# A three-layer hybrid on one core: the residual kept in the output and added to by the last stores, with the filter loop's buffers, filter banks and frequency chunks laid out anew

## Chip, cores and metric

The kernel runs on one core of one Trainium2 chip. The metric is device time of one execution in microseconds (us), the median over several runs. All numbers are float32.

## The reference, cut to what matters

The input is x of 8 × 32 × 32 × 128, which is 8 sequences of 1024 tokens with 128 channels. Three layers run over it, each adding to its input: an attention layer (4 heads of 32), a state-space layer that runs forwards and backwards, and a spectral filter layer (STU). The change touches the end of the second layer and the third. The third layer takes the normalised tokens u and computes, beside three taps of regression on u, a causal convolution of u with 16 spectral filters, each followed by a 128 × 128 matrix, once with u and once with u of alternating sign:

```python
U_plus, U_minus = _stu_conv(phi, u, PADDED_SL)          # FFT convolution, K = 16 filters
s = sigma ** SIGMA_POW
out = jnp.einsum('btkd,k,kde->bte', U_plus, s, Mpp)
out = out + jnp.einsum('btkd,k,kde->bte', U_minus, s, Mpm)
...
out = out + jnp.einsum('btd,de->bte', ui, Mu[i])        # three taps, i = 0..2
```

Which of four banks of matrices is used follows from a gate, and so does a mask `keep` over the positions.

## The kernel before, in words

Everything that counts stands in `fast_kernel` (`general_kernel` runs only if a check on the attention's denominators fails). X[b], the tokens of sequence b with all that has been added to them so far, lives in SBUF, 4 KB per partition, for all 8 sequences.

**Order of the work.** A tile framework places buffers in pools and inserts waits. A buffer that is laid on the bytes of an earlier one waits for the earlier one's last reader, and that may be a store. Within a `manual_schedule` the engines named in it run in program order: in the state-space part all five engines (`ALL_IN_ORDER`), in the two filter stages TensorE, VectorE, ScalarE (ACT) and GpSimd (POOL) (`IN_ORDER`), while SP, which issues nearly all DMAs, is ordered by the framework.

**First filter stage** (L1558 to L1627), a loop over b from 2 to 8. For each sequence `transform(b)` turns the normalised tokens by TensorE (`cpt`, L561), computes their spectra at 128 frequencies as matrix products (`pf`, L571; copied by ACT, L579; summed by VectorE and POOL, L582 to L589) and stores them to `ud` in DRAM (L592). `taps_of(b - 1, k)` computes the regression for each half k (`pu`, L601), and VectorE adds it into X (L611). `store_residual` (L614) then stores X[b] to the DRAM tensor `xa`. In between, `turned(n)` for n = 0 to 3 brings one quarter of the filter matrices (8 of 32, `md`) into SBUF (L1568), turns it on TensorE (`mdt`, L1573), copies it (L1574), and stores it to `me` in DRAM (L1577). After the fourth, four DMAs (L1580) load `me` with the filter index on partitions, as `mst`. Sequences 0 and 1 have had the same done to them earlier, within the state-space part, and X[7] is re-loaded in another layout by `reload(u)` at L1542.

**Second filter stage** (L1629 to L1744), a loop over c, 16 chunks of 8 frequencies. `matrices(c + 1, n, ...)`, for n = 0 to 7, makes the chunk's 128 × 128 matrices from `taps` and `mst`: 16 products into four PSUM banks (`pg`, L1644), which VectorE (L1655) and ACT (L1657) copy by turns into `gs`. `loaded_spectra` (L1664) loads the chunk's spectra `u`, and POOL makes a second form of them (L1667, L1668). `apply` multiplies spectra and matrices (`py`, L1678), `gather` forms sums on ACT and VectorE (L1693 to L1699) and stores them to `yd` (L1701), 4 frequencies per store, so that partition p of the sums is one (frequency, block, sequence, part). `fetch(c)` (L1709) brings the first part of what the tail reads back into `early_yt`, with the frequency on partitions. TensorE's order within an iteration is: two groups of the next chunk's `matrices`, one `apply`, four times. Both `gs` and `u` come from a pool of two buffers that is opened after the first stage's pools and X are released, so that gs0 lies on bytes of X.

**Tail** (L1747 to L1784). When the last chunk begins, `load_residuals` (L1712) brings part of the residuals `xa` back to SBUF; the rest follows in the tail. Six loads of 1 MB (L1753, `room<-yd`) bring the frequencies' sums, partition = frequency. For each of four pieces (block, half of the sequences) VectorE forms z (L1759), TensorE applies the inverse transform (`pz`, L1769), VectorE multiplies by `keep` and adds the residual (L1776), and ACT's queue issues the store to `out` (L1779); the last piece is stored in two parts.

The frequencies have the order 1, 3, 5, ...: `odd` (L326) counts them on one row, and `alt` (L393) holds a sign that alternates from one to the next.

Of the kernel before, what the change touches and what calls it, by code (L numbers as in the profile page):

```python
# [8 lines left out]
F32 = mybir.dt.float32  # L9
# [5 lines left out]
P = 128  # L15
# [30 lines left out]
def fast_kernel(ctx: ExitStack, tc: tile.TileContext, a: dict, out: bass.AP, bad: bass.AP):  # L46
# [27 lines left out]
    xa = dram.tile([B, P, NB, 4, C], F32, name="xa")  # L74
    md = dram.tile([P, 2, KF, C], F32, name="md")
    me = dram.tile([P, 2 * KF, P], F32, name="me")
# [243 lines left out]
    def transforms(pool, tables):  # L320
# [5 lines left out]
        odd = counted(pool, [2, NF], [[512, 2], [2, NF]], 1, 0, "odd")  # L326
# [31 lines left out]
    def transform_taps(pool, ps, tables):  # L358
# [34 lines left out]
        alt = pool.tile([P, NF // 2, 2], F32, name="alt")  # L393
        nc.gpsimd.memset(alt, 1.0)
        nc.gpsimd.memset(alt[:, :, 1], -1.0)
        alt = alt.rearrange("p f i -> p (f i)")
# [215 lines left out]

    def store_residual(b):
        nc.sync.dma_start(xa[b].rearrange("p k r c -> p (k r) c"), X[b])  # L614
# [315 lines left out]
    with ExitStack() as s:  # L930
# [611 lines left out]
        reload(u)  # L1542
# [10 lines left out]
    with ExitStack() as s:  # L1553
        mp = s.enter_context(tc.tile_pool(name="c_m", bufs=1, side="right"))
        mst = mp.tile([P, 32, C], F32, tag="mst", name="mst")
        early_yt = mp.tile([P, 2, 4, 4, C], F32, name="early_yt")

        with ExitStack() as s2:  # L1558
            p1 = s2.enter_context(tc.tile_pool(name="f_1", bufs=1))
            p2 = s2.enter_context(tc.tile_pool(name="f_2", bufs=2))  # L1560
            ps_f = s2.enter_context(tc.tile_pool(name="f_ps_f", bufs=2, space=PSUM))
# [3 lines left out]
            def turned(n, pool, tag, size):  # L1565

                t = p2.tile([P, 8, C], F32, tag="md", name=f"md{n}")
                nc.sync.dma_start(t, md.rearrange("d r k e -> d (r k) e")[:, n * 8 : n * 8 + 8, :])  # L1568
                to = p2.tile([P, 8, C], F32, tag="me", name=f"me{n}")
                for at in range(0, 8, size):  # L1570
                    pt = pool.tile([P, size, C], F32, tag=tag, name=f"mdt{n}_{at}")
                    for i in range(size):
                        nc.tensor.transpose(pt[:, i, :], t[:, at + i, :], ident)  # L1573
                    nc.vector.tensor_copy(  # L1574
                        to[:, at : at + size].rearrange("p k d -> p (k d)"), pt.rearrange("p k d -> p (k d)")
                    )
                nc.sync.dma_start(me[:, n * 8 : n * 8 + 8, :], to)  # L1577
                if n == 3:
                    for g in range(4):
                        nc.sync.dma_start(  # L1580
                            mst[g * 32 : (g + 1) * 32],
                            me[g * 32 : (g + 1) * 32].rearrange("n k d -> k n d"),
                        )
# [23 lines left out]
            s2.enter_context(tc.manual_schedule(engines=IN_ORDER))  # L1607
            uts = {}
            for _ in scaled(3, *third, p2):
                pass  # L1610
            for b in range(2, B + 1):
                if b + 2 < B:
                    norms[b + 2] = normalize(p2, b + 2)
                if b < B:
                    transform(b)
                if 3 < b + 1 < B:
                    for _ in normalized(b + 1, p2, *norms.pop(b + 1), wide=p2):
                        pass
                if b > 2:
                    taps_of(b - 1, 0)  # L1620
                if 2 <= b <= 5:
                    turned(b - 2, *((ps_o, "o", 4) if b == 2 else (ps_t, "t", 8)))
                if b > 2:
                    taps_of(b - 1, 1)
                    store_residual(b - 1)
        middle.close()
        middle.close()  # L1627

        with ExitStack() as s2:  # L1629
            p2 = s2.enter_context(tc.tile_pool(name="g_2", bufs=2))  # L1630
            p3 = s2.enter_context(tc.tile_pool(name="g_3", bufs=3))
            ps_g = s2.enter_context(tc.tile_pool(name="g_ps_g", bufs=8, space=PSUM))

            turn = 0

            def matrices(c, n, gs):

                nonlocal turn
                pts = [ps_g.tile([P, 4, P], F32, tag="g", name=f"pg{c}_{n}_{g}") for g in range(4)]
                cols = slice(c * FC, (c + 1) * FC)  # L1640
                for e in range(4):
                    for g in range(4):
                        rows = slice(g * 32, (g + 1) * 32)
                        nc.tensor.matmul(  # L1644
                            pts[g][:, e, :],
                            lhsT=mst[rows, n * 4 + e, :],
                            rhs=taps[rows, cols].rearrange("p f q m i -> p (f q m i)"),
                            start=True,
                            stop=True,
                        )  # L1650
                for g, pt in enumerate(pts):
                    to = gs[:, :, n * 16 + g * 4 : n * 16 + g * 4 + 4]
                    frm = pt.rearrange("p e n -> p n e")
                    if turn % 2:
                        nc.vector.tensor_copy(to, frm)  # L1655
                    else:
                        nc.scalar.copy(to, frm)  # L1657
                    turn += 1

            def loaded_spectra(c):  # L1660

                u = p2.tile([P, 2, NB, B, 2, 4 * FC], F32, tag="u", name=f"u{c}")
                for k in range(NB):
                    nc.sync.dma_start(  # L1664
                        u[:, 0, k].rearrange("p b i f -> p b (i f)"), ud[c][:, :, k].rearrange("p b i q f -> p b (i q f)")
                    )
                nc.gpsimd.tensor_scalar(u[:, 1, :, :, 0, :], u[:, 0, :, :, 1, :], -1.0, None, ALU.mult)  # L1667
                nc.gpsimd.tensor_copy(u[:, 1, :, :, 1, :], u[:, 0, :, :, 0, :])  # L1668
                return u
# [16 lines left out]
            def gather(c, n, turn, py):  # L1686
# [9 lines left out]
                if turn == 0:  # L1696
# [3 lines left out]
                at = c * FC + n * 4  # L1700
                nc.sync.dma_start(  # L1701
                    yd[at : at + 4].rearrange("f k b i q e -> (f k b i) (q e)"), sums.rearrange("p q e -> p (q e)")
                )

            def fetch(c):

                rows = slice(c * FC, (c + 1) * FC)
                for i in range(2):
                    nc.sync.dma_start(early_yt[rows, i], yd[rows, 0, 0:4, i])  # L1709

            def load_residuals(k, b, n):
                nc.sync.dma_start(  # L1712
                    res[k][:, b : b + n].rearrange("p b r c -> p b (r c)"),
                    xa[b : b + n, :, k].rearrange("b p r c -> p b (r c)"),
                )

            chunks = NF // FC
            gs, us, gathered = {}, {}, {}
            s2.enter_context(tc.manual_schedule(engines=IN_ORDER))
            for c in range(-1, chunks):  # L1720
                if c + 1 < chunks:
                    gs[c + 1] = p2.tile([P, P, C], F32, tag="gs", name=f"gs{c + 1}")
                    us[c + 1] = loaded_spectra(c + 1)
                else:

                    room = p2.tile([P, P, C], F32, tag="gs", name="room")
                    res = [room[:, :32, :], mp.tile([P, 32, C], F32, tag="mst", name="res1")]
                    res = [t.rearrange("p (b r) c -> p b r c", b=B) for t in res]
                    load_residuals(1, 0, B)
                    load_residuals(0, 0, 4)  # L1730

                for n in range(4):
                    if c + 1 < chunks:
                        matrices(c + 1, 2 * n, gs[c + 1])
                        matrices(c + 1, 2 * n + 1, gs[c + 1])
# [13 lines left out]
            for n, (k, h) in enumerate(pieces[1:], 1):  # L1749
# [4 lines left out]
                if n == 2:  # L1754
                    load_residuals(0, 4, 4)
# [835 lines left out]
```

## Time and profile before

| what | us |
|---|---|
| median of 3 runs (lowest, highest) | 1395.06 (1393.53, 1397.17) |
| the profiled execution's own time | 1403.45 |
| its span in the profile | 1401.6 |
| mean granted TensorE clock over the span | 0.98 |
| first filter stage, from its first products (L561) to the last taps (L601) | 997.4 to 1068.4 |
| second filter stage, from the first pg to the last py | 1069.2 to 1356.3 |
| tail, from the first pz to the end of the span | 1363.9 to 1401.6 |
| TensorE busy in 1110 to 1340 | 224.1 of 230 |

The profile is of one execution, and times in it are counted from the start of the span. "Busy" sums the times in which an engine executes; a TensorE that is busy need not be at its peak rate, and the trace lists a float32 product in two passes, so that 16 products stand as 32 records. The chain of waits goes back from the last instruction, each time to what released it; a stretch of it is work, a DMA, or "issue", where the engine waited for nothing that the profile shows. "PEld" is TensorE's loading of weights, "SPq" and "ACTq" are the queues on which DMAs are issued. The granted clock is the share of TensorE's full clock that it was given.

### The profile page before, as it was taken

The numbers are of one execution on the slowest core, as the hardware profiler recorded it, in microseconds if no ns is written. First come the engines' busy times: TensorE is split into PE (matmuls) and PEld (weight loads), VectorE is DVE, ScalarE is ACT, GpSimd is POOL, SyncE is SP. The second block draws the span as 40 slices with busy tenths as digits, with TensorE's granted clock in tenths as the row PEclk, the third lists the DMA queues.
The fourth block names the chain that finished last, engine by engine and source line by source line (L and its number), as shares of the span: only waits on it lengthen the run. The fifth ranks groups of instructions, "written<-read, shape, count | busy, mean of one in ns | idle before, by whom it ended". The sixth has DMA issues, their size and how long they took to land. (4 is left out here: it accounts for less than half of the span.)

```text
span 1401.6 us, 47569 instructions
## 1 busy us (share of the span) xinstructions
PE 1330.1 (95%) x20926; PEld 844.7 (60%) x20926; DVE 1103.4 (79%) x2145; ACT 922.8 (66%) x1428; POOL 536.0 (38%) x510
## 2 busy tenths in 40 slices
PE   7999999999999999999999999998898999999967
PEld 4333333333333666666666666667797988888964
DVE  5789888788778688988889898999564777777745
ACT  5666666766756888888878888876353555555520
POOL 3412986876910343434343343444673011111100
PEclk9999999999999999999999999999999999999979
DMA  7100111111101434444444343431668132222357
GB/s 172 55 2 2 38 39 39 53 39 39 31 1 42 96 78 93 108 94 113 94 108 94 92 95 88 114 83 48 197 208 198 46 78 73 77 69 70 83 171 294
DMA packets 139391, 123.24 MB, mean 88 GB/s; under 512 B 44808, under 2 KB 118152, under 8 KB 135080
## 3 DMA queue, kind: packets, MB, share of 16 engines
q1 hardware_dynamic: 137048, 115.93, 32.0%
q8 instruction: 166, 2.72, 0.8%
q10 hardware_dynamic: 2128, 4.19, 0.8%
q14 instruction: 49, 0.40, 0.1%
HBM read 78.15 MB, written 34.08 MB: 80 GB/s over the span
## 5 line engine op out<-in xcount | busy, mean ns | idle before, releaser
L809 ACT ACTIVATE pr<-pt 128x1024 f32<-128x1024 f32 x256 | 248.2, 1022 | 105.0 <-PE pt L804 103.9
L1657 ACT COPY gs<-pg 128x512 f32<-128x512 f32 x256 | 133.1, 603 | 75.6 <-PE pg L1644 58.4
L1655 DVE COPY gs<-pg 128x512 f32<-128x512 f32 x256 | 159.1, 685 | 26.0 <-PE pg L1644 18.9
L834 DVE TENSOR_TENSOR two<-pr,pr 128x1024 f32<-128x1024 f32 x128 | 164.8, 1328 | 15.2 <-ACT pr L809 15.2
L804 PE MATMUL pt<-q,k 32*128 32x512 f32 x1024 | 162.5, 651 | 6.1 <-ACT pr L809 4.1
L1644 PE MATMUL pg<-taps,mst 32*128 32x128 f32 x4096 | 150.1, 283 | 11.9 <-issue 5.8
L1644 PEld LDWEIGHTS pg<-taps,mst 32*128 32x128 f32 x4096 | 135.0, 189 | 27.2 <-issue 19.3
L825 PE MATMUL po<-pr,v 128*32 128x512 f32 x1024 | 140.6, 610 | 0.0
L1678 PE MATMUL py<-gs,u 128*32 128x128 f32 (+1 forms) x4096 | 130.9, 281 | 3.4 <-issue 3.4
L1030 POOL TENSOR_TENSOR ec<-ec,ct 128x2048 f32<-128x2048 f32 x16 | 83.6, 5224 | 112.3 <-ACT ct L1110 57.1
L1072 DVE SCALAR_TENSOR_TENSOR xs<-xp,cw,xs 128x1024 f32<-128x1024 f32 x96 | 122.5, 1283 | 2.2 <-issue 0.2
L1678 PEld LDWEIGHTS py<-gs,u 128*32 128x32 f32 (+1 forms) x4096 | 114.8, 141 | 10.9 <-issue 3.6
L1094 PE MATMUL pb<-bxt,wbc 128*128 128x512 f32 x256 | 114.0, 597 | 3.6 <-ACT zs L1085 3.6
L1667 POOL TENSOR_SCALAR u<-u 128x512 f32<-128x512 f32 x16 | 24.0, 1499 | 237.5 <-DMA u<-ud 138.3
L804 PEld LDWEIGHTS pt<-q,k 32*128 32x128 f32 x1024 | 49.5, 185 | 88.9 <-ACT pr L809 27.1
L1193 DVE SCALAR_TENSOR_TENSOR state<-state,dec,pst 128x64 f32<-128x64 f32 x448 | 87.3, 275 | 1.1
L1302 POOL TENSOR_TENSOR rms<-rms_v,mhalf 128x8 f32<-128x8 f32 x16 | 26.5, 1659 | 157.0 <-DVE rms_v L1300 157.0
L1094 PEld LDWEIGHTS pb<-bxt,wbc 128*128 128x128 f32 x256 | 47.1, 189 | 60.3 <-issue 55.0
L825 PEld LDWEIGHTS po<-pr,v 128*32 128x32 f32 x1024 | 27.8, 110 | 89.7 <-issue 86.4
L1016 POOL TENSOR_TENSOR lm<-cs,lm 128x2048 f32<-128x2048 f32 x16 | 57.9, 3620 | 57.7 <-DVE xs L1072 22.6
L845 PE MATMUL pd<-two,ones 128*32 128x512 f32 x512 | 74.1, 618 | 2.3 <-DVE two L834 2.1
L1272 PEld LDWEIGHTS spo<-wo,y 128*128 128x128 f32 x512 | 62.1, 191 | 13.1 <-issue 8.9
(310 smaller groups left out, 2784.5 us busy)
## 6 DMA issues: line engine op xcount, KB each, us to landing
lm<-cd SPq DMA_DIRECT2D x32, 512.0 KB
ec<-cd SPq DMA_DIRECT2D x32, 512.0 KB
ud<-sp SPq DMA_DIRECT2D x8, 1024.0 KB
u<-ud SPq DMA_DIRECT2D x32, 256.0 KB
yd<-sums SPq DMA_DIRECT2D x32, 256.0 KB
moved<-state SPq DMA_DIRECT2D x48, 128.0 KB
room<-yd SPq DMA_DIRECT2D x6, 1024.0 KB
X<-in_x SPq DMA_DIRECT2D x8, 512.0 KB
```

Of the source, the lines that this page charges most:

```text
L804: nc.tensor.matmul(pt[:, i, :], lhsT=k[rows, j * P : (j + 1) * P], rhs=q[rows, cols], start=True, stop=True)
L809: nc.scalar.activation(pr[:, 2 * g : 2 * g + 2, :].rearrange("p i t -> p (i t)"), pt.rearrange("p i t -> p (i t)"), AF.Exp, scale=SCALE,)
L825: nc.tensor.matmul(po[rows, :], lhsT=vs[b][:, j, rows], rhs=pr[:, h, :], start=(j == 0), stop=(j == NT - 1))
L834: nc.vector.tensor_tensor(two, sums["pr"][:, 2 * g : 2 * g + 2, :], pr[:, 2 * g : 2 * g + 2, :], ALU.add)
L1030: t = nc.gpsimd.tensor_tensor(u.ec, u.ec, u.ct.unsqueeze(1).to_broadcast([P, NH, NT, L]), ALU.mult)
L1072: u.convolved = nc.vector.scalar_tensor_tensor(acc, xp[:, at : at + T], cw[u.d][:, n, i : i + 1], acc, ALU.mult, ALU.add)
L1094: nc.tensor.matmul(u.pb[:, i * 512 : (i + 1) * 512], lhsT=wbc[u.d][:, k, :], rhs=xt[:, at : at + 512], start=(k == 0), stop=(k == KC - 1),)
L1193: nc.vector.scalar_tensor_tensor(u.state[:, k, h, :], u.state[:, k - 1, h, :], u.dec[:, c, h, j : j + 1], u.pst[c][:, j, h, :], ALU.mult, ...
L1644: nc.tensor.matmul(pts[g][:, e, :], lhsT=mst[rows, n * 4 + e, :], rhs=taps[rows, cols].rearrange("p f q m i -> p (f q m i)"), start=True, ...
L1655: nc.vector.tensor_copy(to, frm)
L1657: nc.scalar.copy(to, frm)
L1678: nc.tensor.matmul(py[t * 32 : t * 32 + 32 - 16 * m, q // 2, :], lhsT=u[:, i, m:, :, :, q * FC + f].rearrange("p k b i -> p (k b i)"), rhs ...
```

## The change

- **Residual in the output.** `xa` is gone. `store_residual` writes X[b] to its place in `out`, and keeps the store's handle. In the tail nothing is loaded; ACT (for r below 2) and VectorE (else) multiply pz by `keep` into the buffer, and the store is issued from POOL's queue with `accum_op=ALU.add`, so that it adds to what stands in `out`. It is made to wait for the residual's store.
- **Bank loads and turns.** Three banks are loaded at the stage's start, the fourth in the first `turned`; SP is in program order as well. `reload` of X[7] moves behind the first of these loads. A turn is done for b = 3 to 6 (it was 2 to 5), all in the same PSUM pool.
- **Banks strided.** A quarter n holds the matrices n, n + 4, n + 8, ..., and `me` is laid out by quarter. `spread(n)` loads quarter n as soon as it is stored, at b = 4 to 7, by four DMAs to every fourth partition, where four DMAs to 32 partitions each stood after the last.
- **Chunks strided.** Chunk c holds the frequencies c, c + 16, c + 32, ...; `odd` and `alt` count accordingly. `yd`'s store goes to four rows 16 apart, `fetch` reads every 16th row into every 16th partition.
- **Buffers apart.** gs and u of even chunks lie in a pool of their own, opened before the first stage; those of odd chunks in one opened after it. Spectra of chunk 0 are loaded at the end of the first stage, and two of its eight groups of `matrices` run there, in two PSUM tiles of two banks each: one before the last half of the last taps, one after. The tail's z uses the u buffers, `early_yt` has a pool of its own.

```diff
-        odd = counted(pool, [2, NF], [[512, 2], [2, NF]], 1, 0, "odd")
+        odd = counted(pool, [2, NF // FC, FC], [[512, 2], [2, NF // FC], [2 * NF // FC, FC]], 1, 0, "odd")
...
     def store_residual(b):
-        nc.sync.dma_start(xa[b].rearrange("p k r c -> p (k r) c"), X[b])
+        residuals[b] = nc.sync.dma_start(
+            out[b].rearrange("(k p r) c -> p k (r c)", k=NB, r=4), X[b].rearrange("p (k r) c -> p k (r c)", k=NB)
+        )
...
         add_rows(u)
-        reload(u)
...
+        first_gs = s.enter_context(tc.tile_pool(name="c_g", bufs=1, side="right"))
...
+            def load_bank(n):
+                mds[n] = pm.tile([P, 8, C], F32, tag="md", name=f"md{n}")
+                nc.sync.dma_start(mds[n], md.rearrange("d r k e -> d (r k) e")[:, n::4, :])
+
+            def turned(n):
+
+                if n == 0:
+                    load_bank(3)
+                pt = ps_t.tile([P, 8, C], F32, tag="t", name=f"mdt{n}")
+                for i in range(8):
+                    nc.tensor.transpose(pt[:, i, :], mds[n][:, i, :], ident)
                 to = p2.tile([P, 8, C], F32, tag="me", name=f"me{n}")
...
+                nc.vector.tensor_copy(to.rearrange("p k d -> p (k d)"), pt.rearrange("p k d -> p (k d)"))
+                nc.sync.dma_start(me[:, n], to)
+
+            def spread(n):
+                for g in range(4):
+                    nc.sync.dma_start(
+                        mst[g * 32 + n : (g + 1) * 32 : 4],
+                        me[g * 32 : (g + 1) * 32, n].rearrange("n k d -> k n d"),
                     )
...
-            s2.enter_context(tc.manual_schedule(engines=IN_ORDER))
+            s2.enter_context(tc.manual_schedule(engines=ALL_IN_ORDER))
+            uts, mds = {}, {}
+            for n in range(3):
+                load_bank(n)
+                if n == 0:
+                    reload(units[-1])
+            gs, begun = {0: chunk_matrices(0, first_gs)}, set()
+
+            def double_banks(n):
+                pts = [ps_f.tile([P, 2, 4, P], F32, tag="f", name=f"pg0_{n}_{i}") for i in range(2)]
+                begun.add((-1, n))
+                matrices(0, n, gs[0], [pts[g // 2][:, g % 2] for g in range(4)])
...
+            planned = {(B, 1): 1, (B, 2): 1}
...
             for b in range(2, B + 1):
+                if 4 <= b <= 7:
+                    spread(b - 4)
...
                 if b > 2:
                     taps_of(b - 1, 0)
-                if 2 <= b <= 5:
-                    turned(b - 2, *((ps_o, "o", 4) if b == 2 else (ps_t, "t", 8)))
+                ahead(b, 1)
+                if 3 <= b <= 6:
+                    turned(b - 3)
                 if b > 2:
                     taps_of(b - 1, 1)
                     store_residual(b - 1)
+                ahead(b, 2)
+            us = {0: loaded_spectra(0, first_gs)}
...
-                at = c * FC + n * 4
+                at = c + n * 4 * chunks
                 nc.sync.dma_start(
-                    yd[at : at + 4].rearrange("f k b i q e -> (f k b i) (q e)"), sums.rearrange("p q e -> p (q e)")
+                    yd[at :: chunks][:4].rearrange("f k b i q e -> f (k b i) (q e)"), sums.rearrange("p q e -> p (q e)")
                 )
...
-                rows = slice(c * FC, (c + 1) * FC)
+                rows = slice(c, NF, chunks)
...
-                    gs[c + 1] = p2.tile([P, P, C], F32, tag="gs", name=f"gs{c + 1}")
-                    us[c + 1] = loaded_spectra(c + 1)
+                    if c >= 0:
+                        gs[c + 1] = chunk_matrices(c + 1, second_gs if c % 2 == 0 else first_gs)
+                        us[c + 1] = loaded_spectra(c + 1, second_gs if c % 2 == 0 else first_gs)
...
-                    load_residuals(1, 0, B)
-                    load_residuals(0, 0, 4)
...
-                if n == 2:
-                    load_residuals(0, 4, 4)
...
-                        nc.vector.scalar_tensor_tensor(
-                            to[:, :, r, :], po, keep[:, blk : blk + 1], to[:, :, r, :], ALU.mult, ALU.add
-                        )
-                    nc.scalar.dma_start(
+                        if r < 2:
+                            nc.scalar.activation(to[:, :, r, :], po, AF.Identity, scale=keep[:, blk : blk + 1])
+                        else:
+                            nc.vector.tensor_scalar(to[:, :, r, :], po, keep[:, blk : blk + 1], None, ALU.mult)
+                    t = nc.gpsimd.dma_start(
                         out[h * 4 + b : h * 4 + b + size, blk * 512 : (blk + 1) * 512].rearrange(
                             "b (p r) c -> p b (r c)", r=4
                         ),
                         to.rearrange("p b r c -> p b (r c)"),
+                        accum_op=ALU.add,
                     )
```

## The prediction

> **What bounds the kernel now.** I read the page first: TensorE is busy nearly everywhere.
>
> ```profile
> span 1401.6 us, 47569 instructions
> PE 1330.1 (95%) x20926; PEld 844.7 (60%) x20926; DVE 1103.4 (79%) x2145; ACT 922.8 (66%) x1428; POOL 536.0 (38%) x510
> ```
>
> So there is little to win inside a stage, and I went to the chain of waits, read in order of time (start, length, what held the chain), from the stage the change begins in.
>
> ```profile
> 999.19 1.75 PE pf L571 x8
> 1000.95 6.92 DMA md<-md
> 1008.00 1.94 PE mdt L1573 x8
> ...
> 1068.42 0.76 DVE X L611
> ...
> 1069.60 5.75 DMA xa<-X
> ...
> 1076.45 12.06 PE pg L1644 x250
> 1088.50 1.95 PE py L1678 x63
> ...
> 1340.87 5.43 PE py L1678 x178
> 1346.29 3.37 issue
> 1349.66 6.63 PE py L1678 x132
> ...
> 1357.57 2.40 DMA yd<-sums
> ...
> 1359.99 3.53 DMA early_yt<-yd
> ...
> 1363.87 30.76 PE pz L1769 x80
> ```
>
> The chain is TensorE but for four holes: a load of a filter bank (1000.95), the store of the last residual (1069.60), a stall for no data ("issue", 1346.29), and the store and re-load of the last frequencies (1357.57 to 1363.87). Between 1088.5 and 1340.9 nothing but TensorE stands in it. Third, the busy times by stretch around the "issue" hole (length, then busy PE, PEld, DVE, ACT, POOL; granted clock; DMA share; GB/s):
>
> ```profile
> 1342.00:1346.20 4.20, 4.20 (x156) 4.02 (x149) 1.76 (x7) 0.53 (x2) 0.00 (x0) 1.00 1.01 324
> 1346.20:1349.70 3.50, 0.13 (x6) 0.03 (x5) 0.00 (x0) 0.00 (x0) 0.00 (x0) 0.82 1.03 377
> 1349.70:1356.40 6.70, 6.58 (x132) 6.31 (x131) 1.38 (x6) 0.57 (x3) 0.00 (x0) 0.58 0.45 163
> ```
>
> The DMA engines are full exactly there, with the residual loads of L1712 (issued at 1340.9 and 1344.6), and after the hole the granted clock is 0.58. TensorE's instructions arrive as 16 KB packets on the instruction queue: all through the loop one starts every 4.1 to 5.3 us, but after 1338.72 the next starts at 1347.19. So the stall is a late packet of instructions behind 2 KB residual packets.
>
> **The change, part by part.** Times are in the profiled execution (span 1401.6, its own time 1403.45 us). The median of the runs is 1395.06, 8.4 lower; I take the differences over unchanged.
>
> A. *Bank load early.* Today `turned(0)` stands between `transform(2)` and `transform(3)` in TensorE's order, and waits. In the changed order `cpt3` follows `pf2` (ends 1002.9) directly; it still needs the PSUM tile that ACT copies out until 1004.5. So it starts at 1004.5, not 1009.7. The clock also stays up: mdt, cpt and pf take 1.94, 1.91 and 4.86 at 0.80 to 0.86, but 1.04, 1.04 and 3.62 at full clock. From there I add full-clock rows (0.87 a turn, 3.46 pf, 2.68 per half of the taps): the last iteration starts at 1004.5 + 4 × 10.56 + 9.7 = 1056.5, today at 1063.06. **Gain 6.5.** Late next would be xn3 (ACT ends it at 1000.8, before it is needed) or POOL (8.3 us of work per 10.56). SP is now in program order, past `reload` and the stores: the first bank's load goes out as today, and `reload` waits as today for the store of X7.
>
> B. *Chunk 0 early.* Today the last taps end at 1068.42, evictions to gs wait for `xa<-X` to land (gs lies on X's bytes), and py starts at 1088.43: 20.0. Afterwards gs0 lies elsewhere, and two of its eight groups run in double banks, one of them (1.08 of TensorE) between the last two halves of the taps. After the taps one group remains, then a bank wait of 1.3, then eight groups (two of chunk 1) at the eviction's pace: VectorE copies two banks in 1.22 to 1.29, as in the row of 12 copies in 7.27 us from 1082.42. 1.1 + 1.3 + 8 × 1.2 = 12.0. **Gain 20.0 − 12.0 − 1.1 = 6.9.** Cover: gs1 lies on X's bytes, and is first written some 9 us after the taps; the last store to `out` should land after about 5. u0 loads behind that store: about 6 to land, 2.1 on POOL (1.51 + 0.60), also before 12.
>
> C. *Banks spread one by one.* Sixteen DMAs of 8 partitions and 128 KB replace four of 32 partitions. The first pg waits for all. A transfer uses at most as many engines as it has rows, by two rows of the trace: first a fetch pair of 8 rows each, then a store of 128 rows.
>
> ```profile
> DMA packets 80, 0.13 MB, mean 57 GB/s; under 512 B 16, under 2 KB 16, under 8 KB 80
> DMA packets 144, 0.26 MB, mean 154 GB/s; under 512 B 16, under 2 KB 16, under 8 KB 144
> ```
>
> The small packets close a transfer, one per engine: 8 for each fetch, 16 for the store. So a bank has 128 packets of 512 B on each of 8 engines: 3.5 us at 27 ns (as ud stores take), 5.8 at 45 ns (as today's mst loads take). Per iteration those engines carry also ud (3.8), me (1.3) and out (1.4): 10 to 12.3 in 10.56. At 27 ns the last bank lands about when pg wants it; at 45 the backlog makes pg some 9 late. **Loss 1**, ends 0 and 9; I stand near 0 because today's loads go to 32 partitions with 16 engines and are likely held by their destination.
>
> D. *The loop.* TensorE's work is the same. But `yd` stores now have 4 rows at the destination: by the same closing packets 4 engines, each 32 packets of 86 ns = 2.75 us instead of 0.74. An instruction packet runs on one engine and does not mix with the transfer in front of it (a 128-row store that meets one has its last 8 packets a whole packet later). In 230 us of loop TensorE is idle 5.9 today, nearly all "issue". With 32 stores, one engine in four, and 2.75 of each 4.1 us in which an instruction packet can fall behind a store for 1.4 on average: 32 × 0.25 × 0.67 × 1.4 = 7.5; today's share by the same sum is 2.1. The phase is locked, so it may miss: **loss 3**, ends −4 (today's stalls fall away) and 9.
>
> The Trainium skill, "DMA: Bandwidth & Descriptors", section "Rules for kernel authors", speaks against this edit: to use all 16 engines an outermost dimension should be a multiple of 16. By it C and D stand on their dear sides, 8 + 6 = 14 us worse; the closing packets agree on the engines, and only a run tells what that costs.
>
> E. *No residual loads.* Three of the 4 MB leave 1341 to 1353. The 256 records of the last chunk's py took 15.4 (5.43 + 3.37 + 6.63); at the loop's 1.95 per 64 they take 7.8. **Gain 7**, between 0 (the hole has another cause) and 7.6.
>
> The skill's "Runtime: NRT & Kernel Launch", "Instruction fetch mechanics", holds that crossing to a new 16 KiB block is mostly hidden; by it E would be 0. The row of 3.37 stands against it, so I keep 7.
>
> F. *Last store and fetch.* yd on 4 engines: 2.75 instead of the 1.3 seen. **Loss 1.5**, ends 0.5 and 2.
>
> G. *Tail.* TensorE's 30.8 stays: it runs on without a gap, ACT and VectorE share evictions (16 a side or less, 0.6 to 0.75) and VectorE's z adds (2.49 a piece) are as now. The 4 MB of loads that go save nothing, since room's pieces come ahead of need. What counts is after the last pz: 0.48 eviction, a store that starts to move 0.9 after issue and takes 1.4 to 3.2, and closing instructions. The new store is issued by POOL and adds in DRAM; no row shows one. From below: as today's, 0. From above: the sum must be read before it is written, 512 KB more at today's 348 to 390 GB/s (1.4) with a round trip like `yd<-sums` (2.4), a POOL issue as dear as POOL's dearest instruction (5.2): 9. I take the read and half a round trip, **loss 3**. POOL's branch at the end then follows its last issue.
>
> Sum: 6.5 + 6.9 − 1 − 3 + 7 − 1.5 − 3 = 11.9; 1395.06 − 11.9 = 1383.2, say **1383**.
>
> **Rivals.**
> 1. *Adding stores are the bound (slower than before).* They start about 10 us into the tail; 4 MB at rate r must end beyond 37.7 + 15 after its start for the gains to be eaten: 4.19 MB / 42 us, so below 100 GB/s. At 80: 52 us, 10 us more, 1405. For it: read, add and write in one pass, descriptors made by POOL. Against: 2 KB packets, and plain ones move at 390. 8%.
> 2. *The narrow transfers cost their dear ends:* C at 9 and D at 6 take 11 from the sum: 1394. For it: 45 ns mst packets, stalls already due to transfers. Against: slack of a half iteration. 15%.
> 3. *The change doesn't do what it says at the seam:* gs1 or u0 waits for the stores as gs0 did, B is 1: 1389. For it: a wait of 5.75 for the same bytes today. Against: one group less to store and 9 us of cover. 12%.
> 4. *Everything cheap:* C 0, D −2, G 0: 1374. 10%.
>
> My forecast has 55%, between 1378 and 1389.
>
> **How the numbers follow.** 0.3% is 4.2 us, about what a measurement tells from no change. Slower by more: rival 1, 8%. Within: half of rival 2 and a little else, 8%. Faster: 84%. The range goes from rival 4's time to rival 2's: 1374 to 1394; left out are rival 1 and about half of each of these two, some 2 in 10.
>
> **What would show it.** A: no DMA in the chain before mdt, mdt after a half of the taps. B: 12 us from the last taps to the first py. C: pg's first wait on `mst<-me` under 2. D: idle TensorE between the first and last py near 9 in 230. E: no "issue" in the last chunk, clock 1.00. F: 2.8 of packets in the last yd. G: under 10 from the last pz to the end. I am wrong if out<- stores trail the last pz by more than 10, or if pg waits for mst.

## The result, and the profile after

The changed kernel takes 1399.45 us in the median of 16 runs (1394.41 to 1405.48), the kernel before 1397.68 in the median of 16 on the same chip (1392.96 to 1402.30). The ratio is 1.0011, with a 95% interval of 0.9996 to 1.0026: no change that can be measured, where 12 less was forecast. Of the 16.5 between the forecast of 1383 and the median, 2.6 lie in the base, since the 1395.06 that the forecast started from was the median of 3 runs.

The profiled execution of the changed kernel has an own time of 1398.45 and a span of 1396.7, so it lies 1.0 below its median. The one of before that the prediction was worked on (1403.45) lies 5.8 above its own. A stretch may therefore be compared between the two profiles only where its length is steady, and I show further down which ones are. First the head of the page, after:

```profile
span 1396.7 us, 47588 instructions
PE 1322.1 (95%) x20926; PEld 839.7 (60%) x20926; DVE 1098.7 (79%) x2134; ACT 928.2 (66%) x1438; POOL 544.1 (39%) x515
```

TensorE has the same number of products as before. Next, the chain of waits of the changed kernel (start, length, what held the chain); L601 is still the taps, L1584 the pg products, L1714 py, L1797 pz:

```profile
1043.63 2.68 PE pu L601 x24
...
1047.18 3.47 PE pf L571 x16
...
1050.96 6.79 DMA me<-me
...
1059.26 4.15 DMA mst<-me
...
1066.33 4.62 PE pu L601 x24
...
1334.07 8.97 PE py L1714 x320
...
1345.21 8.01 DMA yd<-sums
...
1353.27 2.51 DMA early_yt<-yd
...
1356.03 30.26 PE pz L1797 x80
```

Three of the four old holes are gone: no bank load at the stage's start, no store of the last residual in front of pg, and one unbroken 8.97 for the last chunk. Two things stand in their place. The last quarter's store and load (`me<-me`, `mst<-me`) now hold the chain from 1051 to 1063, and the half of the taps behind them takes 4.62 where a half takes 2.68. And `yd<-sums` takes 8.01 where it took 2.40. At the end, 10.4 lie between the last pz and the end of the span; it was 7.0.

### The profile page after: what moved, and what is told of

Its sections match the earlier page's. It is cut to its first block, busy times and chain, and to the rows that moved or that the text cites. A ratio compares the mean times of both kernels' runs of the same rounds, so it can differ in the third digit from the quotient of the medians.

```text
span 1396.7 us, 47588 instructions
## 1 busy us (share of the span) xinstructions
PE 1322.1 (95%) x20926; PEld 839.7 (60%) x20926; DVE 1098.7 (79%) x2134; ACT 928.2 (66%) x1438; POOL 544.1 (39%) x515
## 5 line engine op out<-in xcount | busy, mean ns | idle before, releaser
L838 DVE TENSOR_TENSOR two<-pr,pr 128x1024 f32<-128x1024 f32 x128 | 164.0, 1322 | 13.4 <-ACT pr L813 13.4
L1584 PE MATMUL pg<-taps,mst 32*128 32x128 f32 x4096 | 149.1, 280 | 10.2 <-issue 4.3
L1584 PEld LDWEIGHTS pg<-taps,mst 32*128 32x128 f32 x4096 | 134.3, 187 | 25.0 <-issue 16.7
L1714 PE MATMUL py<-gs,u 128*32 128x128 f32 (+1 forms) x4096 | 127.8, 277 | 0.6 <-DVE gs L1595 0.4
L1714 PEld LDWEIGHTS py<-gs,u 128*32 128x32 f32 (+1 forms) x4096 | 112.0, 141 | 8.2 <-DVE gs L1595 1.5
L1030 ACT ACTIVATE lm<-lm 128x1024 f32<-128x1024 f32 x64 | 65.7, 1052 | 6.8 <-POOL lm L1020 6.6
```

What stands on the lines that cost most here:

```text
L838: nc.vector.tensor_tensor(two, sums["pr"][:, 2 * g : 2 * g + 2, :], pr[:, 2 * g : 2 * g + 2, :], ALU.add)
L1584: nc.tensor.matmul(pts[g][:, e, :], lhsT=mst[rows, n * 4 + e, :], rhs=taps[rows, cols].rearrange("p f q m i -> p (f q m i)"), start=True, ...
L1714: nc.tensor.matmul(py[t * 32 : t * 32 + 32 - 16 * m, q // 2, :], lhsT=u[:, i, m:, :, :, q * FC + f].rearrange("p k b i -> p (k b i)"), rhs ...
```

## The experiments

Every kernel was compared with runs of the kernel before on the same chip. Such runs spread by about 1% (for both kernels), so that the medians bear a few microseconds and the profiles have to say where they lie. This table has the lengths of the stretches in each kernel's profile, in us ("last chunk's remaining py" is the stretch from the last pg to the last py, "idle ahead of pz" the one from there to the first pz):

| kernel | own time | first cpt of the stage to first py | loop: first py to last pg | last chunk's remaining py | idle ahead of pz | last pz to end |
|---|---|---|---|---|---|---|
| before | 1403.45 | 91.0 | 252.4 | 15.4 | 7.6 | 7.0 |
| before_again | 1408.02 | 89.8 | 260.2 | 13.5 | 7.3 | 6.3 |
| tail_only | 1407.14 | 91.0 | 259.7 | 9.5 | 6.7 | 11.7 |
| strided_only | 1409.06 | 90.3 | 254.3 | 12.7 | 10.6 | 6.6 |
| after | 1398.45 | 86.9 | 250.4 | 8.9 | 13.0 | 10.4 |
| after_again | 1403.12 | 87.2 | 252.8 | 9.1 | 13.1 | 11.7 |
| no_add | 1397.09 | 87.6 | 252.0 | 9.1 | 12.9 | 6.8 |
| chunks_back | 1401.54 | 87.4 | 258.7 | 9.7 | 6.9 | 11.0 |
| spread_apart | 1391.46 | 84.5 | 250.3 | 9.7 | 12.5 | 10.3 |
| spread_chunks | 1393.40 | 84.7 | 251.7 | 9.4 | 7.0 | 10.9 |
| no_early | 1394.52 | 81.6 | 252.1 | 8.9 | 13.3 | 10.7 |
| two_back | 1395.29 | 77.9 | 252.9 | 8.9 | 13.4 | 11.6 |
| own_queue | 1394.15 | 77.9 | 255.9 | 9.6 | 9.9 | 10.4 |
| three_back | 1388.50 | 77.9 | 255.8 | 9.1 | 6.9 | 10.7 |
| half_plain | 1390.28 | 77.9 | 255.7 | 9.4 | 6.7 | 8.5 |

Read it by columns. Kernels that share the code of a stretch repeat its length within 1 to 1.5 us, but for two columns: the last chunk where it has a hole in it (12.7 to 15.4), and the loop, which spreads over 10 and differed by 7.8 between two executions of one kernel (before).

### Was the hole in the last chunk there by chance?

before_again: no edit.

> The kernel before, unchanged, for a second profile. Theory 1 (the narrow transfers ate the gains, and the removal of the residual loads is a real gain): the hole of some 3 us of 'issue' in the last chunk's py stands in this profile too, those 256 products take 13 to 16 us, and own time is anywhere between 1393 and 1402. Theory 2 (the hole came by chance in the execution that was profiled): this profile has no such hole, the last chunk's products take 8 to 9 us, and own time lies near 1393 to 1396, so that step E is worth far less than 7 in the median.

Its chain of waits over the last chunk:

```profile
1347.87 5.43 PE py L1678 x185
1353.30 2.25 issue
...
1359.28 1.65 issue
```

The hole is there again, in two parts (3.9 in sum), so theory 2 falls. Its own time, though, was 1408.02 on a chip where 20 runs of before had a median of 1404.52 (1393.96 to 1411.58): it is outside what I gave, because the loop was 7.8 longer.

### The tail's part alone

```diff
 # before, with only this of the change
-        nc.sync.dma_start(xa[b].rearrange("p k r c -> p (k r) c"), X[b])
+        residuals[b] = nc.sync.dma_start(out[b]..., X[b]...)
...
-                    load_residuals(1, 0, B)
-                    load_residuals(0, 0, 4)
...
-                    nc.scalar.dma_start(
+                    t = nc.gpsimd.dma_start(
...
+                        accum_op=ALU.add,
```

> The kernel before with only the residual's part of the change: the residual is stored to out, no residual loads, adding stores from POOL's queue; banks, chunks, buffers, loop as before. Theory (E a gain of some 6, G a loss of some 3): the last chunk's 256 products take 9 to 10 instead of 15.4 and 13.5, from the last pz to the end 10.3 to 11 instead of 7.0 and 6.3, time 2 to 4 below before, ratio 0.997 to 0.999. Rival (the stall is one of instruction supply and comes elsewhere when the residual loads are gone, or the adding stores cost more than 4): ratio 1.000 to 1.004.

Ratio 0.9973 (0.9945 to 1.0002). The last chunk takes 9.5:

```profile
1346.90 5.43 PE py L1681 x182
1352.34 0.17 issue
1352.51 3.93 PE py L1681 x132
```

So the hole goes with the loads (step E), and the end comes 11.7 after the last pz (step G), 0.7 more than I had given: both go the way that the theory has, and they nearly cancel.

### What makes the adding stores dear

```diff
-                        accum_op=ALU.add,
```

> The changed kernel with the tail's stores left as they are (from POOL's queue) but without accum_op: they overwrite, so that the output holds the filter's part alone and the sum with the residual is left out. Theory (the adding makes G dear: an adding 2 KB packet takes 178 ns where a plain one takes 84 to 88, and the stores are a backlog on the engines that ends 10 to 11 after the last pz): packets back at 84 to 90 ns, from the last pz to the end 7 to 8 instead of 10.4 and 11.7, time 3 to 4 below the changed kernel, ratio to before 0.999. Rival (POOL's issue of 1.2 a store and its closing instructions are what is late): the packets are faster but the end stays 10 or more after the last pz, time as the changed kernel's.

Ratio 0.9988 (0.9963 to 1.0012), median 1398.16; the end comes 6.8 after the last pz. What the DMA queues did while the stores ran, first in the changed kernel (1377 to 1387.5), then without the adding (1376.2 to 1379.8), then in the kernel before (1389 to 1391.5):

```profile
DMA packets 1046, 2.08 MB, mean 198 GB/s; under 512 B 32, under 2 KB 32, under 8 KB 1046
q0 software_dynamic: 1046, 2.08, 112.6%
```

```profile
DMA packets 306, 1.13 MB, mean 314 GB/s; under 512 B 30, under 2 KB 30, under 8 KB 306
q0 software_dynamic: 303, 1.13, 82.5%
```

```profile
DMA packets 464, 0.95 MB, mean 380 GB/s; under 512 B 0, under 2 KB 0, under 8 KB 464
q10 hardware_dynamic: 464, 0.95, 101.8%
```

The share is of 16 engines. In the first, 1.126 × 16 × 10.5 us / 1046 = 0.18 us per packet of 2 KB, and the engines are full: the adding stores are a backlog that only ends at 1394.5. In the second the engines are not full, and the packets are of 4 KB (0.825 × 16 × 3.6 / 303 = 0.16 us for each). In the third a plain packet of 2 KB takes 0.088. POOL issues in the first two, so the issue is not the price; the adding is.

### Chunks contiguous again

```diff
-                at = c + n * 4 * chunks
+                at = c * FC + n * 4
...
-                    yd[at :: chunks][:4]...
+                    yd[at : at + 4]...
-                rows = slice(c, NF, chunks)
+                rows = slice(c * FC, (c + 1) * FC)
```

(and `odd` and `alt` as before.)

> The changed kernel with the frequency chunks contiguous again (odd, alt, the store to yd and the fetch as before); all else as changed. Theory 1 (stores of 4 rows pile up at the end of the loop): TensorE's idle time ahead of the first pz falls from 13.0 to about 7.6 us, the last yd store lands in 2.4 instead of 8.0, and time falls by 5 to 7, to about 1393. Rival (the stores' width does not matter, the time is set by the fetch of the last frequencies behind them): idle time stays above 11 and time stays within 2 of 1399.5. A third possibility, that the loop between is made better by the stride (250.3 against 252.4 before): then 2 of the gain is given back, 1395 to 1396.

The chain now has this ahead of pz:

```profile
1352.81 2.04 DMA yd<-sums
...
1354.90 3.25 DMA early_yt<-yd
```

Idle time falls from 13.0 to 6.9, as theory 1 says; ratio 0.9946 (0.9919 to 0.9972), median 1396.46 where before had 1404.52. The loop took its long time in this profile (258.7), and that hid the gain there.

### The strided chunks alone, put on before

The same edit turned round, on the kernel before.

> The kernel before with only the chunks strided (odd, alt, the store to yd, the fetch). Step F seen in the profiles: the idle time ahead of pz 12.5 to 13.3 instead of 7.3, a loss of 5 to 6. Step D in the median is what is asked: if narrow stores cost the loop my 3, ratio 1.006; if nothing, 1.004; if they make it steadier and shorter by 5, as the first profiles look (250.3 to 252.8 against 251.7 to 260.2), ratio 0.999 to 1.001 and a loop of 250 to 253 in the profile.

Ratio 1.0037 (1.0014 to 1.0060), 5.2 us. The idle time rose by only 3 (10.6, where I had 12.5 to 13.3), but the products of the tail took 34.2 instead of about 31 and the hole was a little shorter (12.7). These stretches make up some 4.5 of the 5.2, so little is left for the loop.

### Later on SP

In the changed kernel, SP waits in program order. Its waits over the first filter stage have this line (total, times, longest):

```profile
SPq L1625 <- DMA me<-me: 13.0, 4, 4.1
```

So each time SP stands still until the quarter just stored has landed, and the next spectra and the next store stand behind it.

```diff
-                if 4 <= b <= 7:
-                    spread(b - 4)
+                if b == 7:
+                    spread(3)
...
                     turned(b - 3)
+                    if b > 3:
+                        spread(b - 4)
```

> The changed kernel with only the place of three issues on SP moved: the loads of a quarter into mst are issued one half of an iteration later, so that SP no longer stands still until the same quarter's store to me has landed. Same transfers, same 8 partitions each. Theory 1a (order on SP): SP's 13.0 us of waits for me<-me go down to 3 or less, the last quarter's store to me is issued at 1045 to 1047 instead of 1051, its load lands before 1059, pg waits less than 1 us for mst, and time falls by 7 to 9, to about 1391. Theory 1b (8 partitions, 8 engines: the transfers themselves are too slow): the last load still lands after 1063, the sum of the waits for mst stays above 3, and time stays within 2 of 1399.5.

Neither theory held. The waits of SP for `me<-me` are down to one of 0.4, but the first py comes only 2.7 earlier (84.5 for 87.2), ratio 0.9966 (0.9938 to 0.9994). The last load of a quarter lands 64.7 after the first cpt instead of 66.7, for the store and the load take long here as well:

```profile
1041.85 7.63 DMA me<-me
...
1051.74 5.10 DMA mst<-me
```

Why these two take so long, no run separates. The timeline of TensorE shows what the late landing does (idle time ahead in brackets), and below it the windows (the column after the busy times is the granted clock):

```profile
1054.35 0.48 PE L1584 MATMUL pg<-taps,mst 32*128 32x128 f32 x2 [0.31 <-DMA mst<-me]
1055.20 0.48 PE L1584 MATMUL pg<-taps,mst 32*128 32x128 f32 x2 [0.37 <-DMA mst<-me]
1056.08 0.60 PE L1584 MATMUL pg<-taps,mst 32*128 32x128 f32 x2 [0.39 <-DMA mst<-me]
1056.89 2.07 PE L1584 MATMUL pg<-taps,mst 32*128 32x128 f32 x26 [0.21 <-DMA mst<-me]
1058.89 4.96 PE L601 MATMUL pu<-m_u,ut 128*128 128x128 f32 x24
1063.78 1.17 PE L1584 MATMUL pg<-taps,mst 32*128 32x128 f32 x32
1066.95 9.71 PE L1584 MATMUL pg<-taps,mst 32*128 32x128 f32 x256 [2.00 <-DVE gs L1595]
```

```profile
1054.00:1056.00 2.00, 1.00 (x5) 0.58 (x4) 0.75 (x1) 0.00 (x0) 0.00 (x0) 1.00 1.10 303
1056.00:1058.00 2.00, 1.71 (x22) 1.42 (x26) 0.00 (x0) 0.00 (x0) 0.00 (x0) 0.58 1.07 329
1058.00:1060.00 2.00, 2.00 (x19) 1.77 (x16) 0.78 (x2) 1.07 (x2) 0.00 (x0) 0.50 0.79 278
1060.00:1062.00 2.00, 2.00 (x11) 2.00 (x11) 0.51 (x1) 0.00 (x0) 0.00 (x0) 0.50 0.11 35
1062.00:1064.00 2.00, 2.00 (x18) 1.88 (x19) 0.11 (x1) 0.00 (x0) 0.00 (x0) 0.71 0.00 0
1064.00:1066.00 2.00, 0.95 (x32) 0.76 (x28) 1.04 (x2) 1.01 (x2) 0.00 (x0) 1.00 0.22 84
1066.00:1068.00 2.00, 1.05 (x36) 1.05 (x40) 0.89 (x2) 0.06 (x1) 0.00 (x0) 1.00 1.01 252
```

The waits for mst are only 1.3 in all now, but the group still stutters, and the clock falls to 0.50 just when the last half of the taps, which needs nothing of mst, runs behind it: 4.96, where the same timeline lists 2.84 for a half at full clock. That gave a third theory: the place of the early group is what is dear.

The Trainium skill, "TensorE: Matmul & The Clock Gate", section "Why this matters for your kernels", asks for no idle gap of over some 3 us between bursts of products to keep the clock. Here no gap was over 0.4, and the clock fell all the same. A busy share of a half doesn't explain it: from 1064 to 1068 TensorE was busy for half of the time too, with one gap of 2.0, and the clock stayed at 1.00. Busy time also overstates the work of the stutter: the six records ahead of 1056.89 stand for 1.56, and 32 such records take 1.17 at full clock. What the clock follows stays open.

### Both: later on SP and chunks contiguous

> The two edits together: the loads into mst issued later on SP, and the frequency chunks contiguous again. Theory 1 (the two are separate losses of about 8 and 5 to 7): 1385 to 1387, faster than both kernels by 0.8%. Rival (one and the same loss is paid elsewhere, for instance the loop's instruction packets fall into a worse phase, or the adding stores at the end set the time): 1392 or more.

Median 1395.36, ratio 0.9930 (0.9903 to 0.9958). The two stretches are as with each edit alone (84.7 and 7.0), so by the profile the losses are separate; the time came out where I had put the rival (1392 or more), because the first of the two was worth 2.7, not 8.

### Control

after_again: no edit of the changed kernel.

> The changed kernel once more, for a second profile and for its ratio on the chip on which the others are run. If the strided chunks make the loop steadier (theory D+), the loop from the first py to the last pg takes 250 to 252 again, as in both profiles with strided chunks so far (250.4, 250.3), while contiguous ones gave 252.4, 260.2, 258.7 and 251.7. If the two short ones came by chance (rival), it may as well be 255 to 260. Ratio to before between 0.996 and 1.003 either way.

Ratio 1.002 (0.9991 to 1.005). Loop 252.8.

### No early groups

```diff
-            planned = {(B, 1): 1, (B, 2): 1}
+            planned = {}
```

> The changed kernel without the two early groups: planned is empty, and all eight groups of chunk 0 run after the last taps in single banks, as they did before; banks, chunks, buffers and tail as changed. Theory (the early group between the last two halves of the taps is what makes the late load of the last quarter dear: the taps wait behind it, and the stuttering products take the granted clock to 0.50 while the taps run): the last taps end some 53 + 11 = 64 to 65 after the first cpt of the stage instead of 74.2, ten groups follow when the last quarter lands, and the first py comes 78 to 80 after that cpt instead of 87.0; time falls by 6 to 8, to 0.994 of before or a little above. Rival (the groups wait for the same landing anyway and the eight groups cost more than the two early ones saved): the first py stays at 86 to 88 and the time within 2 of the changed kernel's.

Median 1395.23, ratio 0.9945 (0.9918 to 0.9972). The last taps end 64.6 after the first cpt instead of 74.2, and the first py comes at 81.6: 5.6 better, a little less than I gave, since pg still waits for `mst<-me`. The clock falls here too (0.50 from 1064 to 1068), but what runs then is pg and no longer the taps.

### No early groups and later on SP

two_back joins the last two edits.

> The changed kernel with later mst issues and without early groups, chunks strided: beside the run with contiguous chunks in addition (1388.7) it gives D and F once more, without the stutter ahead of the loop. Loop unchanged in the mean: 6 slower, 1394 to 1395, ratio 0.995. Loop 5 shorter by the stride: 1389 to 1390, ratio 0.991. Loop 3 longer: 1397, ratio 0.997. Profile: first py 77 to 79 after the first cpt, 13 ahead of pz, loop 250 to 253 if the stride is what makes it short.

Here is its chain over the seam:

```profile
1052.60 10.73 PE pu L601 x96
...
1064.16 4.17 PE pg L1584 x96
...
1068.34 8.33 PE pg L1584 x218
```

No DMA is in it. Four halves of taps at full clock, then ten groups of pg, and the first py 77.9 after the first cpt, 3.7 earlier than in no_early. Median 1391.43, ratio 0.9942 (0.9920 to 0.9965), nearest to what I gave for an unchanged loop (0.995); the 3.7 of the profile does not show in the medians (0.9945 for no_early), whose intervals are as wide as that.

### Why is the last yd store so late?

SP's timeline in the changed kernel, at the end of the loop (start, length of the issue):

```profile
1329.67 8.22 SPq L1737 DMA_DIRECT2D yd<-sums  x2
1343.24 0.61 SPq L1745 DMA_DIRECT2D early_yt<-yd  x1
1343.94 0.52 SPq L1737 DMA_DIRECT2D yd<-sums  x1
...
1345.21 0.76 SPq L1737 DMA_DIRECT2D yd<-sums  x1
```

The fetch at 1343.24 had to wait for the narrow stores of chunk 14, and both of chunk 15's stores stood behind it: they follow each other within 1.3. On two_back:

```diff
-                nc.sync.dma_start(
+                early = c == chunks - 1 and n == 0
+                (nc.scalar if early else nc.sync).dma_start(
```

> The kernel with strided chunks, later mst issues and no early groups, and in it the first of the last chunk's two yd stores issued from ACT's queue instead of SP's, where it stands behind a fetch that waits for the stores of the chunk before. Theory Fa (two of the narrow stores follow each other within 1.3 us on the same four engines because SP held the first back; a single one takes 2.9): the last store lands 4 to 5 after its issue instead of 8.3, idle time ahead of pz falls from 13.4 to 9 or 10, ratio 0.991 to 0.992 instead of 0.9942. Theory Fb (the four engines are slow for each store and are still busy with the ones before, whoever issues it): idle time stays at 12 or more, time as before the edit.

The last store's step in the chain, first in two_back, then here:

```profile
1340.60 8.32 DMA yd<-sums
```

```profile
1343.22 5.80 DMA yd<-sums
```

Idle time 9.9 instead of 13.4; ratio 0.9932 (0.9901 to 0.9962), too wide to add to that. So of the 6 that the stride costs here, about 3.5 is the order on SP and 3 the width itself: Fa for more than half, with a rest of Fb. strided_only, where SP is not in program order, agrees: 10.6.

### All three undone

three_back is the changed kernel with contiguous chunks, later mst loads and no early groups.

> The changed kernel with contiguous chunks, the loads into mst issued later on SP, and without early groups. Theory (three separate losses: 6 for the narrow stores at the end, 2 to 3 for the order on SP, 6 to 8 for the early group behind the load): the first py 77 to 79 after the first cpt, idle time ahead of pz 7, time some 14 below the changed kernel, ratio to before 0.988 to 0.990, if the loop takes its short time. Rival (the loop with contiguous chunks falls into its long time, 258 to 260, in most executions): ratio 0.993 or above in the median although the profile shows the three gains.

Median 1388.71 where before had 1401.75; ratio 0.9909 (0.9873 to 0.9945), although the loop in its profile was a middling 255.8. The 0.9% are what I had forecast for the change as it was made. The interval leaves the rival's 0.993 open for the size, not for the sign.

### And the last quarter of the tail without adding

```diff
+            kept = yp.tile([P, 4, 4, C], F32, name="kept")
...
+                if 4 <= c < 8:
+                    t = nc.sync.dma_start(
+                        kept[:, c - 4].rearrange("p r c -> p (r c)"),
+                        out[c, 0:512].rearrange("(p r) c -> p (r c)", r=4),
+                    )
...
+                        if size == 2:
+                            nc.vector.scalar_tensor_tensor(
+                                to[:, :, r, :], po, keep[:, blk : blk + 1], to[:, :, r, :], ALU.mult, ALU.add
+                            )
...
+                    if size == 2:
+                        nc.scalar.dma_start(out[...], to...)
+                        continue
```

> The kernel with contiguous chunks, later mst issues and no early groups, and in it the last piece of the tail (four sequences of one block, 1 of 4 MB) done as before: its residuals are loaded from out during chunks 4 to 7 of the loop into a buffer of their own, added by VectorE, and stored plainly from ACT's queue. Theory (the backlog of adding stores sets the end): 3 MB at 178 ns per 2 KB packet on 16 engines take 17 us from about 1361, the last MB takes 2.8, the end comes some 7 after the last pz instead of 10.7, time 3 to 4 below 1388.7, ratio 0.987 to 0.989. Rival (four loads of 256 KB in the loop cost an instruction packet or two, and the end is set by the closing instructions): 1388 to 1391.

Median 1384.82, ratio 0.9878 (0.9841 to 0.9915): faster than both kernels. Against three_back the intervals overlap; the end comes 8.5 after the last pz, not 7; the third MB of adding stores ends only 3.8 after the last pz, and until then it shares the engines with the plain ones.

## Why the prediction was wrong, point by point

- **A, bank load early: right.** The last pf ends 53.9 after the first cpt in the changed kernel; in the four profiles with the bank load as before it ends after 59.5 to 60.2 (mean 59.9). That is 6.0 less; 6.5 was forecast.
- **B, chunk 0 early: right.** From the last taps to the first py 12.7 in every profile with early groups, 12.0 forecast; with the seam of before 19.88 in the mean, so that against 12.74 a gain of 6.0 is left after the moved group's 1.1. But where the prediction saw the early groups as the gain, the buffers were: without early groups it is 13.3. The two groups save 0.6 there and cost 1.1 ahead of it, so they lose 0.5 even where nothing waits.
- **C, banks one by one: the step that failed.** "At 27 ns the last bank lands about when pg wants it; at 45 the backlog makes pg some 9 late. Loss 1." The packets did take 27, yet from the last pf to the last taps the changed kernel takes 20.6 (mean over after, after_again, no_add and chunks_back, which share this code) where before took 10.7; without the moved group's 1.1 that is a loss of 8.8. pg waits 3.8 for `mst<-me`, where under 2 was to show the step right. I had looked at the engines that carry the bank, and not at the queue that issues it: SP, in program order, waits there 13.0 us for the landing of what it has just stored. That is a part only, since without these waits the last load lands 2.0 earlier. And I had priced a late pg as a delay of pg; it stood ahead of a half of the taps and took the clock to 0.50 with it (4.62 for 2.68). Undoing the place brings the first py forward by 5.6, and the order on SP by a further 3.7 in the profiles; together that is C's loss and the 0.5 of the early groups.
- **D, the loop: a loss of 3 isn't shown.** Eight profiles with the stride have 250.3 to 255.9 (mean 252.6), seven without it 251.7 to 260.2 (mean 256.3). The medians of runs don't show such a gain: two_back is 0.33% above three_back, spread_apart 0.36% above spread_chunks, strided_only 0.37% above before, some 5 us, which is about what step F takes; the changed kernel is 0.65% above chunks_back, some 9, which would leave a loss. So I take 0, give or take 3 or 4; this isn't settled. TensorE's idle time in the loop, near 9 by the prediction, was 5.0 in the changed kernel's profile, and 5.9 and 11.4 in the two of before: most of what makes a loop long is idle time that the profile calls "issue".
- **E, no residual loads: right in its cause, too large in size.** Three profiles with the loads have 12.7 to 15.4 for the last products, the twelve without 8.9 to 9.7: 4.6, where I took 7 from the one profile that had the largest hole. A part of the 7 was a wrong count: the stretch has 320 records of py (the chain after shows them, 8.97 for x320) and not 256, so it takes 9.75 and not 7.8 at the loop's pace, and 5.7 was the most that could go. The Trainium skill, "Runtime: NRT & Kernel Launch", section "Instruction fetch mechanics", would have had 0; holes stood in all three profiles with the loads (3.4, 3.9 and 3.1 us of "issue"); in the twelve without them TensorE's holes there are at most 0.3. The traces fit late instructions as the cause: with the loads, an instruction packet of TensorE's queue starts 8.5, 7.4 and 6.9 after the one before it, without them at most 4.9 in this stretch (3.3 to 5.8 in the loops). For this place the runs speak against it.
- **F, last store and fetch: wrong size,** 5.8 for 1.5 (13.0 instead of 7.2). I had the duration of one store, but not that two would queue, since SP holds the first behind a fetch. 3.5 of it is again the order on SP.
- **G, tail: right sign,** 4.3 for 3 (6.66 from the last pz to the end in before's two profiles and strided_only, 10.93 in the ten in which all stores add). The mechanism was rival 1's: adding stores as the bound, at 198 GB/s, above the 100 from which that rival would have eaten all the gain.

With the measured sizes: −6.0 − 6.0 + 8.8 + 0 − 4.6 + 5.8 + 4.3, and −0.6 for pz (30.33 for 30.97), give +1.7. Measured were +1.8 between the medians; so close an agreement is luck, with a loop that is known to 3 or 4. Of the 13.6 by which the sum was off, C makes 7.8 and F 4.3. Rival 2 had C at 9 and D at 6. Its 9 came out by luck: the reason given, packets of 45 ns, was not it, but the order on SP and the place of a group; and the stalls that were to make D dear did not show in the loop. One thing I had also taken for steady, and it wasn't: the loop of one profile.

## What to carry to other kernels

When an engine's DMA queue is put into program order, list for every wait on it what stands behind it, as for a compute engine; the landing of a store that the next load needs is a wait of some 7 us here (6.79 and 7.63 in the two chains). A product that may come late belongs behind the work that does not need it: ahead of it, it delayed that work here and lowered its clock as well. And take the length of a stretch from two profiles before an estimate rests on it.

## What the runs showed of the hardware

- A store that adds to DRAM took 0.18 us per 2 KB packet and 198 GB/s; the plain stores in the tail of before took 0.088 and 380 GB/s.
- The granted clock fell to 0.50 for nearly 7 us after some 3 us of stuttering products, with no idle gap of over 0.4; one gap of 2.0 soon after left it at 1.00.
- The loop, in its two forms, took between 250.3 and 260.2 in 15 profiles; two of one kernel were 7.8 apart at the same granted clock (0.980 over the span), and TensorE's idle time makes 5.5 of it.
- With 3 MB of loads in flight, TensorE stood still for 3.1 to 3.9 us in each of three profiles, without them for at most 0.3 in each of twelve.
